# A first attention whose keys are projected for two heads at once, and whose probabilities are transposed by VectorE and DMA instead of TensorE

## The chip, the cores and the metric

The kernel runs on one core of one Trainium2 chip. The metric is the device time of one execution in microseconds, the median over repeated runs. A core has TensorE (PE; its weight loads are shown as PEld), VectorE (DVE), ScalarE (ACT), GpSimd (POOL) and SyncE (SP), which here only issues transfers. Each engine works through its own instructions in order and waits at semaphores for the others.

## The reference

Four layers, each an attention and a feed-forward network, with a layer norm behind each. Only the first attention matters here: 1024 rows of 256, 16 query heads and 4 key and value heads of 128, a window of 64 keys, and a difference of two softmaxes, one over each half of the head's 128 dimensions.

```python
q = q * cos + _rotate_half(q) * sin
k = k * cos + _rotate_half(k) * sin
...
q1, q2 = (q[..., :sub], q[..., sub:])
k1, k2 = (k[..., :sub], k[..., sub:])
attn1 = jnp.einsum('bhqd,bhkd->bhqk', q1, k1) * scale
attn2 = jnp.einsum('bhqd,bhkd->bhqk', q2, k2) * scale
...
a1 = jax.nn.softmax(attn1.astype(jnp.float32), axis=-1).astype(x.dtype)
a2 = jax.nn.softmax(attn2.astype(jnp.float32), axis=-1).astype(x.dtype)
diff = jax.nn.relu(a1 - lam.reshape(1, H, 1, 1) * a2)
diff = diff / (diff.sum(axis=-1, keepdims=True) + 1e-06)
out = jnp.einsum('bhqk,bhkd->bhqd', diff, v)
out = out.transpose(0, 2, 1, 3).reshape(B, S, H * hd)
return out @ Wo
```

## The kernel before

Eight stages run one after the other; `attn0` is the first. It works in 32 units: for each key head g (0 to 3) the eight row tiles t of 128 rows. A unit takes the four query heads of g for 128 rows, in two blocks b of 64 rows, each against a window of 128 keys, and in two pairs r of heads. Queries and keys lie transposed, with 64 of the head's dimensions on partitions 0 to 63 and again 64 on partitions 64 to 127: the two heads of a pair take one half of the partitions each. So both halves need the same key rows, and before the change the weight Wk is laid out with each 64 columns twice, so that the projection itself fills both halves.

The loop in `attn0` (from L621) makes iteration i out of parts of several units. It writes the order for PE, ACT, DVE and POOL by hand (`in_order`); SP's queue is ordered by the scheduler. In iteration i stand, in this order:
- the PE transposes of unit i - 3 into a PSUM bank (L729) and ACT's copy to `pt` (L731)
- `attn0_probs`, second part, for unit i - 1: three small DVE operations (L700 to L702), four differences (L708) with ACT's relu behind each (L712)
- one piece of work ahead (`operands`, `rotated`): a projection on PE (L154) and its product with the cosine and sine table on DVE (L570 for Q, L572 for K). After two such pieces POOL subtracts and adds (L577, L578). A run of four units holds six pieces, for the next run's K and two pairs of Q: one per iteration and a second one in odd iterations
- for g = 0, V's tile t (`make_values`), and its copies shifted by 64 rows, two transfers on SP
- the values of unit i - 3 (L735) and ACT's copy of them to `ot` (L741)
- the scores of unit i: mask matmuls (L666) and sixteen products of 64 partitions (L676) into a `wide` PSUM tile, DVE's maximum over it (L684), eight exponentials on ACT (L692)
- the second piece ahead, in odd iterations
- `attn0_probs`, third part, for unit i - 1: two small DVE operations (L716, L718) and POOL's product with the reciprocal sums (L720)
- Wo for unit i - 3 (L747) and the sum into x on DVE (L235)

The second attention (`attn1`) already transposes its probabilities in squares of 32 on DVE (`turn_probs`, L276) and moves them to their partitions with transfers on SP (L284). After the units, the layer norm runs in two halves, its output goes to DRAM (`moe_rows`), and the weights of the first experts are loaded (`gu`, `wd`).

Of the kernel before, what the change touches and what calls it, by code (L numbers as in the profile page):

```python
# [28 lines left out]
ALU = mybir.AluOpType  # L29
AX = mybir.AxisListType  # L30

P = 128
T = 1024
NT = T // P
D = 256
NC = D // P
HALF = 512
PAD = 64
# [474 lines left out]
def attn0(k, a):  # L513

    nc = k.nc
    window_masks(k)
    table = k.tile("rope", [P, 2, T])
    wk, wq, wo = [None] * 2, [None] * 4, [None] * 4

    def load_keys(i):
        wk[i] = k.weights(
            [P, NC, 512],  # L530
            a["L0_attn_Wk"][:, i * 512 : (i + 1) * 512].rearrange("(c p) f -> p c f", p=P),
        )

    def load(g):
        cols = slice(g * 512, (g + 1) * 512)
        wq[g] = k.weights(
            [P, NC, 512], a["L0_attn_Wq"][:, cols].rearrange("(c p) f -> p c f", p=P)
        )
        wo[g] = k.weights(
            [P, 4, D], a["L0_attn_Wo"][cols, :].rearrange("(h p) m -> p h m", p=P)  # L540
        )

    load_keys(0)
    for i, n in enumerate(("rope_cos", "rope_sin")):
        nc.sync.dma_start(out=table[:, i, :], in_=a[n])
    load(0)
    wv = k.weights([P, NC, 512], a["L0_attn_Wv"].rearrange("(c p) f -> p c f", p=P))

    lam = k.tile("rope", [P, 4, 2], tag="lam", bufs=1)
    for pair in range(2):  # L550
        nc.sync.dma_start(
            out=lam[pair * 64 : pair * 64 + 64],
            in_=a["L0_attn_lam"].rearrange("(g p r) -> g p r", g=4, p=2)[:, pair, :]
            .unsqueeze(0).to_broadcast([64, 4, 2]),
        )
    nc.vector.tensor_scalar(lam, lam, -1.0, None, ALU.mult)
    load_keys(1)
    load(1)

    def rotated(weight, half, first, second, scale):  # L560

        parts = []
        for i in range(2):
            ps = k.bank()
            k.project(ps, lambda c: weight(i, c), half * HALF, HALF)
            t = k.tile("t", [P, 2, HALF])
            twice = ps.unsqueeze(1).to_broadcast([P, 2, HALF])
            by = table[:, :, half * HALF : (half + 1) * HALF]
            if scale == 1.0:
                nc.vector.tensor_tensor(t, twice, by, ALU.mult)  # L570
            else:
                nc.vector.scalar_tensor_tensor(t, twice, scale, by, ALU.mult, ALU.mult)  # L572
            parts.append(t.rearrange("p i (b n) -> p i b n", n=64))
            if i == 0:
                yield
        x, y = parts
        nc.gpsimd.tensor_tensor(first, x[:, 0], y[:, 1], ALU.subtract)  # L577
        nc.gpsimd.tensor_tensor(second, y[:, 0], x[:, 1], ALU.add)  # L578
        yield

    keys, queries = {}, {}

    def operands(g, half):

        if half == 0:
            keys[g] = [k.tile("k", [P, PAD + T]) for _ in range(2)]
            for kt in keys[g]:
                nc.gpsimd.memset(kt[:, :PAD], 0.0)
        cols = slice(PAD + half * HALF, PAD + (half + 1) * HALF)
        yield from rotated(  # L590
            lambda i, c: wk[g // 2][:, c, (g % 2 * 2 + i) * P : (g % 2 * 2 + i + 1) * P],
            half, *(kt[:, cols].rearrange("p (b n) -> p b n", n=64) for kt in keys[g]), 0.125,
        )

        queries[g, half] = [k.tile("q", [P, 8, 2, 64]) for _ in range(2)]
        for pair in range(2):
            yield from rotated(
                lambda i, c: wq[g][:, c, (2 * pair + i) * P : (2 * pair + i + 1) * P],
                half, *(q[:, :, pair, :] for q in queries[g, half]), 1.0,
            )  # L600

    odd, even = [], []

    def make_values(t):
        vt = k.tile("v", [P, 512])
        ps = k.bank()
        k.project_rows(ps, lambda c: wv[:, c, :], t * P)
        nc.scalar.copy(vt, ps)  # L610
        odd.append(vt)
        vt = k.tile("v", [P, 512])
        if t == 0:
            nc.gpsimd.memset(vt[:64], 0.0)
        else:
            nc.sync.dma_start(out=vt[:64], in_=odd[t - 1][64:])
        nc.sync.dma_start(out=vt[64:], in_=odd[t][:64])
        even.append(vt)

    runs = [(g, half) for g in range(4) for half in range(2)]  # L620
    with k.in_order():  # L621
        for _ in operands(*runs[0]):
            pass
        units = [(g, t) for g in range(4) for t in range(NT)]
        ahead, made = iter(()), {}
        for i in range(len(units) + 3):
            ending = iter(())
            if i >= 3:
                g, t = units[i - 3]
                ending = attn0_values(k, t, g, made.pop(i - 3), (even, odd), wo[g])  # L630
            next(ending, None)
            if i - 1 in made:
                next(made[i - 1])
            if i < len(units):
                g, t = units[i]
                if t % 4 == 0:
                    for _ in ahead:
                        pass
                    at = i // 4 + 1
                    ahead = operands(*runs[at]) if at < len(runs) else iter(())  # L640
                    if t == 0 and 0 < g < 3:
                        load(g + 1)
                next(ahead, None)
                if g == 0:
                    make_values(t)
            next(ending, None)
            if i < len(units):
                made[i] = attn0_probs(k, t, g, queries[g, t // 4], keys[g], lam)
                next(made[i])
                if i % 2:  # L650
                    next(ahead, None)
            if i - 1 in made:
                made[i - 1] = next(made[i - 1])
            for _ in ending:
                pass
# [65 lines left out]
    yield four  # L721


def attn0_values(k, t, g, four, values, wo):

    nc = k.nc
    ps = k.bank()
    for i in range(4):
        nc.tensor.transpose(ps[:, i * P : (i + 1) * P], four[:, i, :], k.ident)  # L729
    pt = k.tile("pt", [P, 2, 2, P])  # L730
    nc.scalar.copy(pt.rearrange("p r b n -> p (r b n)"), ps)  # L731
    yield
    out = k.bank()
    for b in range(2):
        nc.tensor.matmul(  # L735
            out[:, b * 256 : (b + 1) * 256].rearrange("p (r n) -> p r n", r=2),
            lhsT=values[b][t][:, g * P : (g + 1) * P], rhs=pt[:, :, b, :],
            start=True, stop=True,
        )
    oT = k.tile("ot", [P, 4, 2, 64])  # L740
    nc.scalar.copy(  # L741
        oT.rearrange("p h b n -> p b h n"), out.rearrange("p (b h n) -> p b h n", b=2, n=64)
    )
    yield
    y = k.bank()[:, :D]
    for i in range(4):
        nc.tensor.matmul(  # L747
            y, lhsT=oT[:, i % 2 * 2 + i // 2].rearrange("p b n -> p (b n)"), rhs=wo[:, i, :],
            start=i == 0, stop=i == 3,
        )  # L750
    k.add_rows(t, y)
# [1344 lines left out]
def ffn3(k, a):  # L2096
# [46 lines left out]


STAGES = (attn0, ffn0, attn1, ffn1, attn2, ffn2, attn3, ffn3)
SCOPES = {
    attn0: dict(wide=2, mask=1, rope=1, k=4, v=16, q=4, t=4, e=3, diff=4, pt=3, ot=3),
    ffn0: dict(wide=0, gu=1, wd=1, route=8, rows=6, xT=3, s=3, h=3, hT=3, y=4, prep=1),
    attn1: dict(q=2, k=5, v=12, pt=2, p4=2, turned=2, ot=7, bv=1, prep=1),
    ffn1: dict(p4=4, t2=15, parts=2),  # L2150
# [39 lines left out]
def laid_out(inputs):  # L2190

    a = {n: np.asarray(v) for n, v in inputs.items()}
    a["L0_attn_x"] = a["L0_attn_x"].reshape(T, D)
    a["rope_cos"], a["rope_sin"] = rope_tables()


    wq = a["L0_attn_Wq"].reshape(D, 8, 2, 2, 64)
    a["L0_attn_Wq"] = wq.transpose(0, 1, 3, 2, 4).reshape(D, 2048)
    wk = a["L0_attn_Wk"].reshape(D, 4, 2, 1, 64)
    a["L0_attn_Wk"] = np.broadcast_to(wk, (D, 4, 2, 2, 64)).reshape(D, 1024)  # L2200
    for n in ("bq", "bk", "bv"):
        a[f"L1_attn_{n}"] = a[f"L1_attn_{n}"].reshape(16, P).T
    for n in ("w_gate_up", "w_proj"):
# [44 lines left out]
```

## Time and profile before

| | |
|---|---|
| median of three runs | 2282.05 us (2280.4 to 2284.7) |
| the profiled execution | 2276.97 us |
| its span | 2275.3 us |
| mean granted TensorE clock | 0.965 |
| PE busy | 2065.0 us, 91% of the span |
| DVE busy | 1325.2 us, 58% |
| ACT busy | 856.9 us, 38% |
| POOL busy | 528.2 us, 23% |
| first maximum of the first attention (L684) starts | 28.42 us |
| last one starts | 272.32 us |
| last sum into x (L235) starts | 294.04 us |

The times in the table by engine are sums of busy time over the whole span, over stages with different limits. A row of a group gives the line, the engine, the operation, the tile written and the tile read, the shapes, the count, then busy us and mean ns of one, then the idle time of the engine before them and who ended it. The chain of waits follows the work that ended last back from the end: each row is a start, a length and what was running.

### The profile page before, as it was taken

What the parts mean: (1) busy time and instruction counts of PE and PEld (TensorE: products, weight loads), DVE (VectorE), ACT (ScalarE), POOL (GpSimd) and SP (SyncE); (2) the same over time, 40 slices, a digit from 0 to 9 for tenths busy, and PEclk for the clock granted to TensorE, in tenths of its full rate; (3) what the DMA queues carried; (4) which work ended last, traced back from release to release, by engine and by line L of the source; (5) the groups of instructions that cost most, each with busy time, mean ns of one, the idle gap of its engine ahead of it and who ended that gap; (6) DMA issues with size and microseconds to landing.
All of it is one profiled execution on the core that took longest, in us unless ns stands there. A gap on an engine that the chain in (4) does not pass through costs nothing.

```text
span 2275.3 us, 25208 instructions
## 1 busy us (share of the span) xinstructions
PE 2065.0 (91%) x7955; PEld 1211.8 (53%) x7955; DVE 1325.2 (58%) x2687; ACT 856.9 (38%) x2230; POOL 528.2 (23%) x805
## 2 busy tenths in 40 slices
PE   8999769799999997988888999899998778999997
PEld 4666545466676665754434444466666444444443
DVE  5677646567776777456744444476767774222223
ACT  3666624443343433444452224544443321111111
POOL 4333221333333333402110001333333220000000
PEclk9999879899999999979999999999999989999999
DMA  4100054254545544105000010244445441111100
GB/s 160 36 10 29 29 169 121 65 136 110 139 112 151 151 111 117 38 28 177 2 2 10 28 29 1 48 90 111 96 103 112 104 95 39 37 40 44 30 2 19
DMA packets 200804, 166.74 MB, mean 73 GB/s; under 512 B 71680, under 2 KB 176192, under 8 KB 200672
## 3 DMA queue, kind: packets, MB, share of 16 engines
q1 hardware_dynamic: 191088, 140.07, 24.0%
q0 software_dynamic: 9584, 25.05, 3.7%
q8 instruction: 65, 1.06, 0.2%
q14 instruction: 67, 0.55, 0.1%
HBM read 68.72 MB, written 17.17 MB: 38 GB/s over the span
## 4 chain that ended last, share of the span: by engine, by line
PE 67%; DVE 15%; ACT 6%; DMA 4%; issue 4%; POOL 2%; SPq 1%; DVEq 0%; ACTq 0%; POOLq 0%
PE bank L154 23%; PE wide L307 8%; PE wide L332 8%; PE bank L298 7%; PE bank L161 4%; DVE turned L276 3%; ACT e L692 3%; PE bank L758 2%; DMA pt<-turned 2%; PE bank L1107 2%; PE bank L1544 1%; PE bank L938 1%; PE bank L1282 1%; DVE st L684 1%; PE bank L747 1%
## 5 line engine op out<-in xcount | busy, mean ns | idle before, releaser
L154 PE MATMUL bank<-xT,w 128*128 128x512 f32 (+2 forms) x1520 | 659.8, 567 | 4.1 <-DVE xT L180 2.6
L154 PEld LDWEIGHTS bank<-xT,w 128*128 128x128 f32 (+1 forms) x1520 | 287.9, 194 | 272.6 <-issue 250.7
L276 DVE STREAM_TRANSPOSE turned<-p 128x128 f32<-128x128 f32 (+7 forms) x256 | 312.8, 1222 | 122.1 <-DMA pt<-turned 87.0
L307 PE MATMUL wide<-k,q 128*128 128x512 f32 (+3 forms) x768 | 294.1, 493 | 29.6 <-ACT p L253 28.7
L261 POOL TENSOR_SCALAR p<-p,st 128x128 f32<-128x128 f32 (+7 forms) x256 | 190.4, 744 | 503.0 <-DVE st L260 502.5
L298 PE MATMUL bank<-pt,v 128*128 128x256 f32 x1216 | 282.0, 375 | 7.5 <-DMA pt<-turned 5.0
L298 PEld LDWEIGHTS bank<-pt,v 128*128 128x128 f32 x1216 | 231.5, 194 | 61.9 <-issue 20.0
L307 PEld LDWEIGHTS wide<-k,q 128*128 128x128 f32 x768 | 141.2, 191 | 152.2 <-issue 93.6
L248 DVE TENSOR_REDUCE st<-wide 128x1 f32<-128x128 f32 (+7 forms) x256 | 194.1, 758 | 8.8
L253 ACT ACTIVATE p<-wide,st,factor 128x128 f32<-128x128 f32 (+7 forms) x128 | 106.4, 831 | 235.0 <-POOL st L250 223.7
L2138 DVE TENSOR_TENSOR t<-t,bank 128x512 f32<-128x512 f32 (+1 forms) x66 | 45.4, 688 | 251.6 <-PE bank L154 251.0
L332 PE MATMUL wide<-t,w 128*128 128x512 f32 (+1 forms) x392 | 187.3, 600 | 4.5 <-DVE t L2139 2.8
L253 ACT ACTIVATE p<-wide,st 128x128 f32<-128x128 f32 (+7 forms) x128 | 94.9, 741 | 249.5 <-DVE st L248 229.4
L2137 ACT ACTIVATE t<-bank 128x512 f32<-128x512 f32 (+1 forms) x66 | 39.4, 597 | 306.2 <-PE bank L154 306.2
L161 PE MATMUL bank<-w,xT 128*128 128x512 f32 (+3 forms) x320 | 124.6, 525 | 2.9 <-DVE xT L180 2.9
L243 DVE TENSOR_TENSOR wide<-wide,causal 128x128 f32<-128x128 f32 x256 | 74.2, 290 | 89.7 <-PE wide L307 88.5
L332 PEld LDWEIGHTS wide<-t,w 128*128 128x128 f32 (+1 forms) x392 | 68.2, 189 | 108.6 <-issue 48.1
L692 ACT ACTIVATE e<-wide,st 128x128 f32<-128x128 f32 x256 | 90.1, 377 | 50.9 <-DVE st L684 34.4
L1569 ACT ACTIVATE pt<-wide 128x1024 f32<-128x1024 f32 (+3 forms) x96 | 75.7, 811 | 72.2 <-PE wide L1563 69.9
L161 PEld LDWEIGHTS bank<-w,xT 128*128 128x128 f32 x320 | 59.2, 208 | 48.5 <-issue 42.7
L2131 POOL COPY t<-select 99x128 bf16<-99x128 bf16 (+1 forms) x33 | 9.4, 292 | 319.8 <-PE bank L988 319.8
L235 DVE TENSOR_TENSOR x<-bank,x 128x256 f32<-128x256 f32 x120 | 48.1, 412 | 50.6 <-PE bank L747 21.1
(310 smaller groups left out, 2864.0 us busy)
## 6 DMA issues: line engine op xcount, KB each, us to landing
pt<-turned SPq DMA_DIRECT2D x96, 128.0 KB, 2.8
pt<-turned SPq DMA_DIRECT2D x96, 96.0 KB, 2.4
pt<-turned SPq DMA_DIRECT2D x32, 256.0 KB, 4.9
w<-in_L_ffn_gate_up_dram SPq DMA_DIRECT2D x16, 512.0 KB, 3.7
pt<-turned SPq DMA_DIRECT2D x64, 112.0 KB, 2.5
pt<-turned SPq DMA_DIRECT2D x32, 224.0 KB, 4.4
w<-in_L_attn_Wq_dram SPq DMA_DIRECT2D x12, 512.0 KB, 4.3
w<-in_L_attn_Wo_dram SPq DMA_DIRECT2D x12, 512.0 KB, 3.8
```

The costliest lines, as they stand in the source:

```text
L154: self.nc.tensor.matmul(out, lhsT=weight(c), rhs=self.xcols(c, lo, n), start=c == 0, stop=c == NC - 1)
L161: self.nc.tensor.matmul(out, lhsT=self.xcols(c, lo, n), rhs=weight(c), start=c == 0, stop=c == NC - 1)
L243: nc.vector.tensor_tensor(scores[:, n - P : n], scores[:, n - P : n], self.causal, ALU.add)
L248: nc.vector.tensor_reduce(top, scores[:, :n], axis=AX.X, op=ALU.max, negate=True)
L253: nc.scalar.activation(probs[:, :n], scores[:, :n], AF.Exp, bias=top, scale=1.0 if scale is None else scale, accum_out=total,)
L261: self.nc.gpsimd.tensor_scalar(probs[:, :n], probs[:, :n], total, 1.0, ALU.mult, ALU.mult)
L276: nc.vector.transpose(squares[:, slot if both else 0], probs[:, :n].rearrange("p (k i b) -> p b k i", b=4, i=32),)
L298: self.nc.tensor.matmul(out[:, first * P :].rearrange("p (s q) -> p s q", q=32), lhsT=value, rhs=pt[:, first * 4 :, b * 32 : b * 32 + 32], ...
L307: self.nc.tensor.matmul(s[:, lo : lo + m], lhsT=query, rhs=key(lo, m), start=True, stop=True)
L332: nc.tensor.matmul(acc[m][:, half * HALF : (half + 1) * HALF], lhsT=down[:, m * P : (m + 1) * P], rhs=h, start=i == 0, stop=i == count - 1,)
L692: nc.scalar.activation(e[:, r, f, b, :], sc[:, r, f, b, :], AF.Exp, bias=top[:, at : at + 1], accum_out=total[:, at : at + 1],)
L1569: nc.scalar.activation(two[:, :, lo:], sc[:, :, lo:], AF.Exp)
```

## The change

There are three parts.

K: Wk is laid out without the doubling, so one projection holds one half of the dimensions of two key heads, one on each half of the partitions. `rotated` is called for K only when g is even, and makes both heads' keys; POOL subtracts and adds for each head on its own 64 partitions (four operations in place of two). Four transfers on SP then copy each head's keys to the other 64 partitions. Wk is one load of 512 KB instead of two, and `k` has six buffers instead of four.

Probabilities: `attn0_turned` is new. It transposes a unit's probabilities in 32x32 squares on DVE, with the rows read at a stride, and four transfers of 64 KB on SP spread the result to `pt`. It is called in iteration i for unit i - 2, after the differences of unit i - 1. The PE transposes and ACT's copy are gone, and the matmul of the values reads `pt` in blocks of 32.

Order: since there is no copy ahead of the values any more, `attn0_values` starts directly with its matmuls, at the place where they stood.

```diff
-    load_keys(0)
+    wk = k.weights([P, NC, 512], a["L0_attn_Wk"].rearrange("(c p) f -> p c f", p=P))
...
-    load_keys(1)
     load(1)
...
         x, y = parts
-        nc.gpsimd.tensor_tensor(first, x[:, 0], y[:, 1], ALU.subtract)
-        nc.gpsimd.tensor_tensor(second, y[:, 0], x[:, 1], ALU.add)
+        for rows, out in first:
+            nc.gpsimd.tensor_tensor(out, x[rows, 0], y[rows, 1], ALU.subtract)
+        for rows, out in second:
+            nc.gpsimd.tensor_tensor(out, y[rows, 0], x[rows, 1], ALU.add)
         yield
...
+        heads = range(g, g + 2) if g % 2 == 0 else ()
         if half == 0:
-            keys[g] = [k.tile("k", [P, PAD + T]) for _ in range(2)]
-            for kt in keys[g]:
-                nc.gpsimd.memset(kt[:, :PAD], 0.0)
...
+        if heads:
+            cols = slice(PAD + half * HALF, PAD + (half + 1) * HALF)
+            own = [slice(j * 64, j * 64 + 64) for j in range(2)]
+            yield from rotated(
+                lambda i, c: wk[:, c, (g + i) * P : (g + i + 1) * P], half,
+                *(
+                    [
+                        (own[j], keys[g + j][f][own[j], cols].rearrange("p (b n) -> p b n", n=64))
+                        for j in range(2)
+                    ]
+                    for f in range(2)
+                ),
+                0.125,
+            )
+            for j in range(2):
+                for f in range(2):
+                    kt = keys[g + j][f]
+                    nc.sync.dma_start(out=kt[own[1 - j], cols], in_=kt[own[j], cols])
...
-            next(ending, None)
             if i - 1 in made:
                 next(made[i - 1])
+            if i - 2 in made:
+                made[i - 2] = attn0_turned(k, made[i - 2])
...
+def attn0_turned(k, four):
+    turned = k.tile("turned", [P, 4, P])
+    k.nc.vector.transpose(
+        turned.rearrange("p b (k q) -> p b k q", q=32),
+        four.rearrange("p k (i b) -> p b k i", b=4),
+    )
+    pt = k.tile("pt", [P, 4, 2, 2, 32])
+    for at in range(4):
+        k.nc.sync.dma_start(
+            out=pt[:, at].rearrange("p r b q -> p (r b q)"), in_=turned[at * 32 : at * 32 + 32]
+        )
+    return pt
...
-    ps = k.bank()
-    for i in range(4):
-        nc.tensor.transpose(ps[:, i * P : (i + 1) * P], four[:, i, :], k.ident)
-    pt = k.tile("pt", [P, 2, 2, P])
-    nc.scalar.copy(pt.rearrange("p r b n -> p (r b n)"), ps)
-    yield
...
-            out[:, b * 256 : (b + 1) * 256].rearrange("p (r n) -> p r n", r=2),
-            lhsT=values[b][t][:, g * P : (g + 1) * P], rhs=pt[:, :, b, :],
-            start=True, stop=True,
+            out[:, b * 256 : (b + 1) * 256].rearrange("p (r a q) -> p r a q", r=2, a=4),
+            lhsT=values[b][t][:, g * P : (g + 1) * P],
+            rhs=pt[:, :, :, b, :].rearrange("p a r q -> p r a q"), start=True, stop=True,
...
-    attn0: dict(wide=2, mask=1, rope=1, k=4, v=16, q=4, t=4, e=3, diff=4, pt=3, ot=3),
+    attn0: dict(wide=2, mask=1, rope=1, k=6, v=16, q=4, t=4, e=3, diff=4, turned=2, pt=3, ot=3),
...
-    a["L0_attn_Wk"] = np.broadcast_to(wk, (D, 4, 2, 2, 64)).reshape(D, 1024)
+    a["L0_attn_Wk"] = wk.transpose(0, 1, 3, 2, 4).reshape(D, 512)
```

More of the change, by code (lines that the diff above doesn't have):

```diff
@@ L525, in attn0 @@
     table = k.tile("rope", [P, 2, T])
[L526 to L532, printed above, removed]
+    wq, wo = [None] * 4, [None] * 4
     def load(g):
@@ L583, in operands @@
     def operands(g, half):
+        heads = range(g, g + 2) if g % 2 == 0 else ()
         if half == 0:
-            keys[g] = [k.tile("k", [P, PAD + T]) for _ in range(2)]
-            for kt in keys[g]:
-                nc.gpsimd.memset(kt[:, :PAD], 0.0)
[L589 to L593, printed above, removed]
+            for j in heads:
+                keys[j] = [k.tile("k", [P, PAD + T]) for _ in range(2)]
+                for kt in keys[j]:
+                    nc.gpsimd.memset(kt[:, :PAD], 0.0)
+        if heads:
[16 more added lines that the diff above has]
+                    nc.sync.dma_start(out=kt[own[1 - j], cols], in_=kt[own[j], cols])
         queries[g, half] = [k.tile("q", [P, 8, 2, 64]) for _ in range(2)]
@@ L598, in operands @@
                 lambda i, c: wq[g][:, c, (2 * pair + i) * P : (2 * pair + i + 1) * P],
-                half, *(q[:, :, pair, :] for q in queries[g, half]), 1.0,
+                half, *([(slice(0, P), q[:, :, pair, :])] for q in queries[g, half]), 1.0,
             )
@@ L721, in attn0_probs, with attn0_values @@
     yield four
-def attn0_values(k, t, g, four, values, wo):
-    nc = k.nc
-    ps = k.bank()
-    for i in range(4):
-        nc.tensor.transpose(ps[:, i * P : (i + 1) * P], four[:, i, :], k.ident)
-    pt = k.tile("pt", [P, 2, 2, P])
-    nc.scalar.copy(pt.rearrange("p r b n -> p (r b n)"), ps)
-    yield
+def attn0_turned(k, four):
[10 more added lines that the diff above has]
+    return pt
+def attn0_values(k, t, g, pt, values, wo):
+    nc = k.nc
     out = k.bank()
@@ L2198, in laid_out @@
     a["L0_attn_Wq"] = wq.transpose(0, 1, 3, 2, 4).reshape(D, 2048)
-    wk = a["L0_attn_Wk"].reshape(D, 4, 2, 1, 64)
-    a["L0_attn_Wk"] = np.broadcast_to(wk, (D, 4, 2, 2, 64)).reshape(D, 1024)
+    wk = a["L0_attn_Wk"].reshape(D, 2, 2, 2, 64)
+    a["L0_attn_Wk"] = wk.transpose(0, 1, 3, 2, 4).reshape(D, 512)
     for n in ("bq", "bk", "bv"):
```

## The prediction

> **What bounds the kernel now.** The change touches only the first attention stage, the first 296 us of the 2275 us span, so I read that stage alone. First its busy times in a table by stretch (the columns are length, then busy us and instruction count of PE, PEld, DVE, ACT and POOL, then the granted TensorE clock, the DMA share and GB/s):
>
> ```profile
> 130.00:165.00 35.00, 32.57 (x187) 21.50 (x186) 27.24 (x55) 23.02 (x119) 13.85 (x12) 1.00 0.00 1
> ```
>
> PE is busy for 93% of this stretch and DVE for 78%. That looks like a PE bound, but an average hides who ends the wait. So next I read the chain of waits of the stage in order of time (start, length, what). Three pieces show three kinds of interval between the exponentials of two units:
>
> ```profile
> 36.67 2.91 ACT e L692 x16
> 40.22 1.14 DVE diff L708 x4
> 41.36 1.13 DVE t L570
> 42.49 1.14 DVE st L684
> ...
> 147.93 2.91 ACT e L692 x16
> 151.08 1.26 DVE st L701
> 152.37 0.97 DVE st L702
> 153.63 0.87 DVE diff L708 x3
> 154.50 1.14 DVE t L572
> 155.64 1.13 DVE st L684
> ...
> 156.86 1.23 ACT e L692 x7
> 158.16 1.61 ACT e L692 x9
> 160.29 1.13 PE bank L735 x4
> 161.75 0.89 PE wide L676 x16
> ```
>
> The first piece is a ring of DVE and ACT: exponentials, 0.64 of small DVE work, difference (1.14), rotation (1.13), maximum (1.17 to the next exponential). It closes in 36.67 to 43.66, that is 6.99 us. The second piece is the same ring, 8.93 us long, because two tiny operations (L701, L702), 0.16 each elsewhere, took 1.26 and 0.97 while POOL was at its rotations and its product. The third goes through PE: exponentials, the copy of the transposed probabilities behind them on ACT, values (L735), scores (L676), maximum: 156.86 to 164.01, 7.15 us. A fourth kind, PE's own queue, takes 7.87. The starts of the 32 maxima (L684) run from 28.42 to 272.32, 243.9 us, and repeat every four units as 8.94, 7.14, 7.87, 7.14 = 31.1. So DVE with ACT and PE are nearly equal rings, and work on DVE is not free.
>
> Third, the groups by line and shape for the prices, and the page's DMA issues for the new transfers:
>
> ```profile
> L570 DVE TENSOR_TENSOR t<-bank,rope 128x1024 f32<-128x1024 f32 x32 | 38.8, 1221 | 9.5 <-PE bank L154 9.5
> L729 PE MATMUL bank<-ident,diff 128*128 128x128 f32 x128 | 20.2, 282 | 0.0
> L731 ACT COPY pt<-bank 128x512 f32<-128x512 f32 x32 | 19.5, 608 | 7.3 <-PE bank L729 7.3
> L276 DVE STREAM_TRANSPOSE turned<-p 128x512 f32<-128x512 f32 x32 | 35.5, 1110 | 13.4 <-DMA pt<-turned 8.5 <-POOL p L261 4.8
> ...
> pt<-turned SPq DMA_DIRECT2D x96, 96.0 KB, 2.4
> ```
>
> L276 is the second attention's transposition by squares, with the same shape and pattern that the change brings to the first: 1.11 us on DVE.
>
> **Removed.** Per unit, the four PE transposes (0.60 together) and ACT's copy (0.61). Of sixteen K projections eight go: 8 x 1.72 = 13.8 us of PE and 8 x 1.22 = 9.8 us of DVE. With the transposes PE loses 20.2 + 13.8 = 34 us. ACT's copy was a link of the 7.15 ring, so that ring disappears.
>
> **Added on DVE.** 32 transpositions. In the order of the changed program each stands after the differences of the unit before and ahead of the rotation and the maximum of the next. That is inside the 6.99 ring. Price 1.11 plus two semaphore waits of 0.05 (seen before L276) = 1.2. The bounds are 0, if PE makes DVE wait there anyway, and 1.2; I take 1.2, since PE is what gets lighter. Behind the transposition wait the rotation, the maximum, ACT's exponentials and PE's later scores. An interval with a rotation becomes 6.99 + 1.2 = 8.2; one without, 8.2 - 1.14 = 7.06.
>
> **Moved on POOL.** K's rotation becomes four operations on 64 partitions in place of two on 128. POOL casts of 64x128 and 128x128 take 0.29 alike, so I price each at the 1.27 of a full one (lower bound half). Total work stays (16 x 1.27), but one block of 5.1 us stands where 2.5 stood. It starts as the rotation ends, 1.1 before the exponentials, and at 40.6 in the clock of the first piece it would still run when L701 wants to start at 39.8, and the product L720 queues behind it. So L701 waits 0.7 and L702 0.9: 1.6 per K block. The Q block at the end of such a run costs the 1.9 seen in the second piece. Without a K block the run has four rotations instead of six, and its last Q block ends before L701: no delay.
>
> **Added on SP.** 128 transfers pt<-turned and 16 copies of K halves; one 512 KB weight load goes. In the second attention SP's issue rows for pt<-turned have a median of 0.60, and the transfer lands 2.4 after the issue begins: 3 x 0.6 + 2.4 and two hand-overs of 0.1, 4.4 after the transposition. Counted back from the next maximum through scores, mask and values (2.25), the values are needed 7.1 after it where the intervals have rotations, and 4.8 after it where they have none. So the latency is covered, by 2.7 and by 0.4 us. The queue behind SP (V's halves, attention weights) stands in an order where each waits for work no later than the transposition that follows it, so I price that at nothing; a 512 KB load ahead of a set could cost 1.7 us, inside the 2.7. K's copies land some 3 us after POOL's block and are used two units later; at the start they fall in the wait for lam (landing at 20.13), so the head stays.
>
> **The sum over the intervals.** By the four units that share a run of rotations, new against old, in us:
> Units 1 to 3: 7.0 + 9.8 + 8.2 = 25.0 against 21.1. Units 4 to 7: 10.1 + 8.2 + 8.2 + 7.06 = 33.6 against 34.9. Units 8 to 11: 31.7 against 31.1. Units 12 to 15: 4 x 8.2 + 1.6 = 34.4 against 31.1. Units 16 to 19: 32.8 + 1.9 + 1.6 = 36.3 against 31.1. Units 20 to 23: 33.6 against 31.4. Units 24 to 27: 31.7 against 30.8. Units 28 to 31, no rotations: 4 x 7.06 = 28.2 against 32.4.
> Together 254.4 against 243.9: +10.5.
>
> **PE's clock.** The last run was dear before for another reason:
>
> ```profile
> 247.00:249.00 2.00, 0.10 (x3) 0.09 (x1) 2.00 (x6) 1.75 (x9) 0.00 (x0) 1.00 0.72 234
> 251.00:253.00 2.00, 1.33 (x6) 0.73 (x4) 1.28 (x6) 1.52 (x7) 0.00 (x0) 0.50 0.00 0
> ```
>
> PE stood for 1.9 us, then ran at clock 0.50, and one interval took 9.59. The excess of the last run over 4 x 7.15 was 3.8. PE will stand still longer there (4.3 of 7.06 busy), so I add 3.8 again; bounds 0 and four times 2.4. The Trainium skill (TensorE: Matmul & The Clock Gate, Part 1: The HAM clock gate) puts the fall of the clock at one idle window of about 3.4 us; here it fell after a gap of 1.9, with shorter ones before. By that rule the gaps I expect (up to 2.4 us) would not throttle at all and the sum would be 3.8 lower.
>
> **Tail.** From the last exponential (273.64) to the last sum into x (294.04) it took 20.4. New, from that exponential: Wo of unit 29 to 8.4, its sum 9.0, the last transposition 10.2, landing 14.5, values, copy and Wo 4.3: 18.9; by way of unit 30, held by 768 KB of expert weights, 19.7. So -1, between -2.5 and +2.
>
> 10.5 + 3.8 - 1 = +13.3. The profiled execution took 2276.97 (span 2275.3 and 1.7 around it), 5 below the median of the runs, 2282.05. On it the sum gives 2290; on the median, **2295 us**.
>
> **Rivals.** (1) Faster: PE is the bound, and DVE waits for scores in any case, so the transposition fits in that wait. For it speak the 93% and the intervals of 7.87 and 9.59; against it, PE's work per unit falls to 6 to 7 us. Without 30 x 1.2 on the ring the sum is 13.3 - 36 + 1.5 (PE then bounds units 4 to 7) = -21: 2261. It decides once the transposition's share on the ring is under 0.76 us a unit (1.2 - 13.3 / 30). (2) Slower still: PE, with more gaps, loses its clock also in the four intervals without a rotation and twice more: 6 x 2.4 = 14 on top, 2309. For it: the clock at 0.50 after 1.9 us; against: 1.00 held from 130 to 245. (3) The transfers are late: at 4.9 us to landing, the page's row for 256 KB, the last run alone gets 4 x 1.2 more, 2300; with SP stalls in ten units 3 us each, 2325. (4) A wash: 64-partition operations on POOL take half and the clock holds: 13.3 - 4.8 - 3.8 = +5, 2287, with a shorter tail 2285.
>
> **The numbers.** This kernel can be told from no change at about 0.2%, 4.6 us. Forecast 0.60 (its own range 2288 to 2302: the clock's 0 to 3.8 and 5 more, the tail's bounds), rival 1 0.09, rival 2 0.12, rival 3 0.07, rival 4 0.12. Faster 0.10 (rival 1 and a little), same 0.13 (rival 4 and the low end of the forecast), slower 0.77. The range 2279 to 2308 leaves out rival 1, the worst of 2 and 3.
>
> **What would show it.** Right: the maxima's starts 8.2 apart with a rotation and 7.1 without, the transposition in the chain between difference and rotation, PE's busy time in the stage down by 34 us with no gain, L701 stretched after K blocks. Wrong: intervals near 7 with DVE idle ahead of the maximum until PE (rival 1); clock rows under 0.9 between 130 and 245 (rival 2); PE's values idle until pt<-turned (rival 3). A head longer by several us, or stages after 300 us that moved, would upset the sum too.

## The result, and the profile after

The changed kernel takes 2282.53 us, the median of 20 runs; the kernel before, beside it, takes 2280.4 us, also of 20. The ratio is 1.0006, 95% interval 0.9997 to 1.0015: no difference that can be told. The forecast was 2295 and slower. The medians differ by 2.1 us, the ratio makes it +1.4. The time lies inside the range given, but a slower kernel was forecast and none can be told; the chance given for that was 0.13.

The profiled execution of the changed kernel took 2287.66 us (span 2285.9). First the table of the same stretch as before (length, then busy us and count of PE, PEld, DVE, ACT, POOL, then PE's clock, DMA share, GB/s):

```profile
130.00:165.00 35.00, 29.33 (x136) 19.40 (x138) 27.66 (x56) 18.87 (x103) 14.12 (x12) 0.90 0.20 47
```

PE's busy share fell from 93% to 84%, and the granted clock, a mean over the stretch, from 1.00 to 0.90. DVE hardly moved (78% to 79%). Now the chain of waits of the stage (start, length, what):

```profile
125.70 2.91 ACT e L703 x16
...
130.38 1.05 DVE turned L740
131.43 1.11 DVE t L565
132.54 1.14 DVE st L695
...
133.76 2.91 ACT e L703 x16
...
136.91 1.00 DVE st L712
...
138.30 0.78 issue
...
143.27 2.91 ACT e L703 x16
```

The transposition (L740) stands in the chain between the differences and the rotation, as forecast. The ring from 125.70 to 133.76 is 8.06 long. It was 6.99, and the transposition with its hand-over is 1.05 of it. The next interval, behind a K block, is 9.51 long: L712 takes 1.00 where the interval before had 0.17, and the chain then shows 0.78 ahead of the last three differences, where it has 0.10 one interval earlier ("issue" is time in which the engine waits for nothing that the profile shows).

The 32 maxima now start from 27.95 to 277.28: 249.33 us against 243.9, +5.4. Summed over the runs of four units, in the order of the prediction: 24.74, 32.35, 31.23, 33.73, 34.77, 32.82, 31.01, 28.67. The tail from the last exponential to the last sum into x is 19.2 against 20.4, so that sum starts at 297.73 against 294.04, +3.7. The prices, from the groups by line and shape and the page's DMA issues:

```profile
L740 DVE STREAM_TRANSPOSE turned<-diff 128x512 f32<-128x512 f32 x32 | 35.1, 1098 | 0.0
L571 POOL TENSOR_TENSOR q<-t,t 128x512 f32<-128x512 f32 x16 | 20.3, 1269 | 70.1 <-DVE t L563 49.0 <-DVE st L727 21.2
L571 POOL TENSOR_TENSOR k<-t,t 64x512 f32<-64x512 f32 x8 | 10.1, 1263 | 25.7 <-DVE t L565 25.4
...
pt<-turned SPq DMA_DIRECT2D x224, 64.0 KB, 2.1
```

One loss in this execution was not seen again. Behind the feed-forward network the chain shows a wait that no other profile of this study has at that place:

```profile
424.82 5.62 another core or an unknown queue
```

The span of this profile is 10.6 us longer than that of the kernel before; the stage of the change makes 3.7 of it and this wait 5.6. A second profile of the same kernel, told below, is without the wait and took 2272.39 us. What it was stays open.

### The profile page after: what moved, and what is told of

It is laid out like the page before. It is cut to its first block, busy times and chain, and to the rows that moved or that the text cites. A ratio compares the mean times of both kernels' runs of the same rounds, so it can differ in the third digit from the quotient of the medians.

```text
span 2285.9 us, 25073 instructions
## 1 busy us (share of the span) xinstructions
PE 2050.6 (90%) x7795; PEld 1198.8 (52%) x7795; DVE 1339.4 (59%) x2711; ACT 840.3 (37%) x2198; POOL 529.6 (23%) x805
## 4 chain that ended last, share of the span: by engine, by line
PE 62%; DVE 19%; ACT 6%; DMA 4%; issue 4%; POOL 3%; SPq 2%; another core or an unknown queue 0%; DVEq 0%; ACTq 0%; POOLq 0%
PE bank L154 21%; PE wide L332 7%; PE wide L307 7%; PE bank L298 7%; DVE turned L276 4%; ACT e L703 3%; PE bank L161 3%; DMA pt<-turned 3%; PE bank L780 2%; PE bank L1566 2%; SPq L284 1%; DVE st L695 1%; DVE turned L740 1%; DVE diff L719 1%; PE bank L1129 1%
## 5 line engine op out<-in xcount | busy, mean ns | idle before, releaser
L154 PE MATMUL bank<-xT,w 128*128 128x512 f32 (+1 forms) x1488 | 647.6, 569 | 6.9 <-DVE xT L180 5.0
L154 PEld LDWEIGHTS bank<-xT,w 128*128 128x128 f32 x1488 | 287.3, 197 | 273.0 <-issue 247.9
L769 PE MATMUL bank<-w,ot 128*128 128x256 f32 x256 | 72.8, 434 | 26.7 <-ACT ot L763 26.6
```

Of the source, the lines that this page charges most:

```text
L154: self.nc.tensor.matmul(out, lhsT=weight(c), rhs=self.xcols(c, lo, n), start=c == 0, stop=c == NC - 1)
```

## The experiments

Theory: the change pays for the transposition in the ring of DVE and ACT, 1.05 us in every unit, and for a longer POOL block behind K; what it earns from PE is no more than that, for PE's rings of 7.14 and 7.87 stood only 0.15 and 0.88 above the ring of 6.99. Rivals: PE or its clock sets the pace (then DVE work is cheap); the landing of the transposed probabilities sets it (then their later use helps); the two halves of the change each do nothing. The kernel before was run again beside each of the three groups of experiments: 2275.32, 2274.46 and 2275.05 us. One per mille is 2.3 us, and a difference in us below is worked out from the ratio, not from two medians.

**The K part alone.** Unit i - 3 keeps its PE transposes and ACT's copy (`attn0_values` is that of the kernel before).

```diff
+            next(ending, None)
             if i - 1 in made:
                 next(made[i - 1])
-            if i - 2 in made:
-                made[i - 2] = attn0_turned(k, made[i - 2])
...
```

> Only the change of K: one projection for two heads, four POOL operations on 64 partitions, copies by SP; the PE transposes and ACT's copy stay as before. Theory A (both halves of the change move the time and cancel): the runs of four units with four rotations instead of six lose their PE-bound interval (7.87) and their POOL delay (1.8), about 2.5 us in each of four such runs; the three K blocks of four POOL operations delay L701 and L702 by 1.5 us each. Together some 6 us faster than before, about 2276 where before is 2282. Theory B (neither half matters, the stage is bound elsewhere): within 2 us of before. Theory C (K's copies by SP are late): PE waits for k ahead of scores, slower.

Measured: 2272.42 us, ratio 0.9986 (0.9971 to 1.0), that is -3.2 us. The maxima span 241.44 against 243.9. Half of what was expected: the 7.87 intervals did not vanish, one is left in most runs of four, and two of 8.76 came in. By the time alone this gain cannot be told from none.

**The transposition alone,** with the old K (`attn0_turned` and `attn0_values` are those of the changed kernel).

```diff
-            next(ending, None)
             if i - 1 in made:
                 next(made[i - 1])
+            if i - 2 in made:
+                made[i - 2] = attn0_turned(k, made[i - 2])
...
```

> Only the transposition by VectorE and SP; K projected for each head as before. Theory A: every interval with a rotation is 8.04 (6.99 + 1.05), all runs have six rotations and one POOL delay of 1.3 to 1.9: 33.5 per four units against 31.1, so 10 us over the stage, 1 us given back in the tail: 9 us slower than before, about 2291 where before is 2282. Theory B (the transposition is hidden): within 2 us of before or faster. Theory C (the transfers bound the stage): more than 20 us slower, with PE's values waiting for pt<-turned in most units.

Measured: 2283.18 us, ratio 1.0037 (1.0023 to 1.0051), +8.4 us. Nearly every run of four is 9.1, 8.05, 8.0, 8.05, and the maxima span 251.73, +7.8. So the halves are opposed, and the cost of this one is clear of the noise: +7.8 and -2.5 on the span of the maxima make +5.3, and the whole change shows +5.4 (+4.4 in its second profile). In the whole time they make +5.2 against +1.4, which their 95% intervals do not tell apart. The third rival is out.

**The transposition done twice.** In `attn0_turned`:

```diff
     k.nc.vector.transpose(turned..., four...)
+    k.nc.vector.transpose(turned..., four...)
```

> The changed kernel, with every transposition on VectorE done twice into the same tile (the second is superfluous). Theory A (the transposition lies whole in the ring of DVE and ACT): 30 intervals longer by 1.03 to 1.07 each, 31 us slower than the changed kernel, about 2313. Theory B (it is hidden behind PE): under 10 us slower.

Measured: 2311.47 us, ratio 1.0162 (1.0134 to 1.019). Against the changed kernel's 1.0006 that is 1.56%, 35 us; the span of the maxima grows by 281.57 - 249.33 = 32.2, or 1.07 for each of 30 units. Its chain of waits:

```profile
133.46 1.06 DVE turned L740
...
134.54 1.10 DVE turned L744
135.65 1.11 DVE t L565
```

The second one stands in the chain at its full length, as the first does. Nothing else was late enough to hide it, so PE does not set the pace of these intervals.

**K's rotation staged.** Two POOL operations on all 128 partitions write a tile `both`, and eight transfers on SP spread it to the keys.

```diff
+            both = [k.tile("both", [P, HALF]) for _ in range(2)]
...
-                *(
-                    [
-                        (own[j], keys[g + j][f][own[j], cols].rearrange("p (b n) -> p b n", n=64))
-                        for j in range(2)
-                    ]
-                    for f in range(2)
-                ),
-                0.125,
+                *([(slice(0, P), s.rearrange("p (b n) -> p b n", n=64))] for s in both), 0.125,
...
-                    kt = keys[g + j][f]
-                    nc.sync.dma_start(out=kt[own[1 - j], cols], in_=kt[own[j], cols])
+                    for rows in own:
+                        nc.sync.dma_start(out=keys[g + j][f][rows, cols], in_=both[f][own[j]])
```

> The changed kernel, but POOL makes the rotated keys of two heads with two operations on 128 partitions into a tile of their own, and eight copies by SP instead of four bring them to their places. Theory A (the long POOL block delays L712 and L713): the three intervals of 9.5 become 8.04, 4.5 us faster than the changed kernel, about 2278 where that is 2282.5; POOL busy 10 us less. Theory B (the 9.5 has another cause, such as K's projection): the intervals stay at 9.5.

Measured: 2271.24 us, ratio 0.9984 (0.997 to 0.9999). Against the changed kernel -0.22%, 5 us. The three intervals behind K blocks fall from 9.53 to 8.0, and POOL's busy time falls by 11.6 us. In the groups the small operation is the changed kernel's L712 (first row) and this kernel's L706 (second):

```profile
L712 DVE TENSOR_TENSOR st<-st 128x4 f32<-128x4 f32 x32 | 9.5, 296 | 1.1
```

```profile
L706 DVE TENSOR_TENSOR st<-st 128x4 f32<-128x4 f32 x32 | 6.5, 202 | 1.1
```

3.0 of the 5 us is this one operation, no longer stretched; most of the rest is the wait of the differences behind it. So the price of the K block lies in POOL's four operations, at full price each.

**The same on the kernel with the K part alone.**

> Before with only K changed and K staged in that way; PE transposes and ACT's copy stay. Theory A: the three intervals of 8.5 of the kernel with K alone become 7.1, 4 us less than that one, so 7 us faster than before. Theory B (the copies of K cost as much as they save): the same as before.

Measured: 2271.32 us, ratio 0.9982 (0.9964 to 1.0): -4.1 against before, 1 better than the K part alone where 4 were expected, and the 95% intervals do not tell the two apart. The delays behind K blocks are gone, but the intervals are 7.15 to 7.87 all the same, with a few of 8.7. Its chain of waits at one of those:

```profile
111.60 0.48 ACT pt L735
...
112.13 2.08 PE bank L739 x4
```

ACT's copy and PE end the wait here, with PE slowed (the same values took 1.13 at 97.11). With the PE transposes left in place, this ring takes over what the others give up.

**The transposition moved, values at i - 3.** The call goes behind the maximum of unit i and the third part of unit i - 1, so that it no longer stands ahead of the next exponentials.

```diff
-            if i - 2 in made:
-                made[i - 2] = attn0_turned(k, made[i - 2])
...
             if i - 1 in made:
                 made[i - 1] = next(made[i - 1])
+            if i - 2 in made:
+                made[i - 2] = attn0_turned(k, made[i - 2])
```

> The changed kernel with the transposition of unit i - 2 moved behind the maximum of unit i on VectorE, under its exponentials, and the values still at i - 3. Theory A (the transposition is in the ring, the transfers are hidden by the 7 us between it and the values): the ring is shorter by 1.05, but the values now need the transfer at once, and it lands 4.1 after the transposition; intervals become 9 to 10 through transfer, values, scores, maximum, 30 to 50 us slower than the changed kernel. Theory B (transfers never matter): 30 us faster than the changed kernel.

Measured, in a single execution: 2379.48 us, some 105 above the kernel before. The direction was expected, the size is twice to three times as large. The chain of waits:

```profile
145.75 1.10 DVE turned L740
...
148.76 2.10 DMA pt<-turned
...
151.00 2.04 PE bank L757 x4
...
154.95 1.23 DVE st L695
```

A new ring: transposition, SP's issues, landing, values, scores, maximum, 10.7 us long from one transposition to the next (156.48); over the stage the maxima stand 11.1 apart in the mean. PE idles in it, its clock over 130 to 165 is 0.75, and the values take 2.04 where the last unit of the changed kernel shows 1.11. That PE slows down in a ring that idles it is a part of the size that was missed: values, mask and scores take some 1.6 more per interval than at full clock.

**The values at i - 4, the transposition where the change put it.**

```diff
-        for i in range(len(units) + 3):
+        for i in range(len(units) + 4):
...
-            if i >= 3:
-                g, t = units[i - 3]
-                ending = attn0_values(k, t, g, made.pop(i - 3), (even, odd), wo[g])
+            if i >= 4:
+                g, t = units[i - 4]
+                ending = attn0_values(k, t, g, made.pop(i - 4), (even, odd), wo[g])
```

> The changed kernel with the values taken from unit i-4 instead of i-3, the transposition left where it was, ahead of the rotation and the maximum. It tells apart what the gain of late_lag4 came from: the place of the transposition or the later use of its result. If the transposition in the ring is the price (my theory), the intervals stay at 8.05 with a rotation and 6.9 without, only the 7.93 of unit 28 may fall to 6.9, the tail grows by one iteration (2 to 4 us), and the time is that of the changed kernel, 2280 to 2286 (ratio to the kernel before 0.999 to 1.003). If the landing of the transposed probabilities is what the changed kernel pays for (rival), the intervals fall towards 7.05 and the time towards 2262 (ratio 0.993).

Measured: 2277.39 us, ratio 1.001 (0.9999 to 1.0021). The intervals stay at 8.04 and 6.9, the span of the maxima at 249.18, and the tail grows from 20.5 to 22.9, counted from the last maximum. Using the result later earns nothing by itself: the second rival is out, the landing was covered in nearly every interval.

**Both: moved, and the values at i - 4.** The edits of the last two together.

> As the kernel before it, but the values, Wo and the sum of a unit one iteration later (i - 4). Theory A: the ring is 7.0 with a rotation and 5.9 without, PE then bounds some intervals at 7 to 7.9, POOL's delays stay; 25 us off the intervals, 2 to 4 given back by a longer tail: 2258 where the changed kernel is 2282. Theory B (the transposition is not in the ring, the loss comes with the transfers or the K copies): within 5 us of the changed kernel.

Measured: 2261.58 us, ratio 0.9928 (0.9902 to 0.9955), -16 us. Against the changed kernel that is -18, where 24 were expected. The intervals fall to 7.05 and 5.91; behind the K blocks they are 8.6, and at the start of most runs of four 8.2 to 10.0. Two of these are PE's: the chain of 9.20 (unit 8) and of 10.04 (unit 24) runs through Wo and a projection on PE, at a granted clock of 0.60 over 204 to 208 and 0.69 over 208 to 214 in the second case (Wo took 3.78 there, 1.73 at full clock in the kernel before). With the transposition out of the ring, PE's slow clock does cost time. The move needs the extra unit of slack, and the slack alone is worth nothing.

**Both, with K staged.**

> The same with the rotated keys of two heads made by two POOL operations on 128 partitions into a tile of their own and copied by SP. Theory A: the three K blocks delay nothing any more, 4.5 us less than the kernel above, about 2254 where before is 2280. Theory B: no gain over before.

Measured: 2251.63 us, ratio 0.9888 (0.9862 to 0.9913), -25 us; it beats both kernels. The maxima span 219.44, 12 less than without the staging where 4.5 were expected; only part of it lies behind K blocks, for unit 24 alone takes 7.05 instead of 10.04, at clock 1.00. That PE kept its clock there is not shown to come from the staging. Its table by stretch and its chain of waits:

```profile
130.00:165.00 35.00, 31.42 (x168) 20.58 (x164) 30.50 (x63) 22.71 (x123) 15.08 (x13) 1.00 0.39 96
```

```profile
132.49 2.91 ACT e L697 x16
...
136.03 1.14 DVE diff L713 x4
137.17 1.13 DVE t L563
138.30 1.14 DVE st L689
...
139.53 2.91 ACT e L697 x16
```

This is the old ring of 6.99 again, 7.04 long. The transposition runs on DVE while ACT takes its exponentials, out of the chain. DVE does one transposition more per interval than in the kernel before and is busy for 87%.

**The changed kernel once more,** for a second profile.

> The changed kernel unaltered, a second profiled execution. By the theory the intervals of the first attention repeat within 0.1 (9.5 to 9.8 behind a K block, 9.1 to 9.3 behind a Q block, 8.05 with a rotation, 6.9 without), the stage's maxima span 249 to 250 us, and the 5.6 us in which the chain waited at 424.8 for something outside the core are not there again. If that wait belongs to the change, it is there again within 2 us of the same place, after the sum into x. Ratio to the kernel before 0.999 to 1.002.

Measured: 2275.32 us, ratio 1.0005 (0.9993 to 1.0018). The maxima span 248.29; most intervals repeat within 0.1 or 0.2, but unit 4 took 10.27 (9.25 in the first profile), unit 20 9.15 (9.85) and unit 28 6.94 (7.93). In unit 4 of this profile PE had first waited for the landing of a transposition (to 48.24), ran at half pace (scores 1.71), and DVE's rotation then waited 1.28 for PE: one place where the transfers and the clock did cost about 1 us. The wait at 424.8 is not there. The last sum into x starts at 297.64 (297.73 in the first profile), but the first gather of the feed-forward network at 317.74, where it was 319.86 and, before, 316.09: PE's clock held longer in the routing between them (0.83 over 301 to 305, against 0.56). So how far the +3.7 reaches varies by 2 us from one execution to the next.

## Why the prediction was wrong, by its steps

The forecast sum was +13.3; the measured place to hold it against is the last sum into x, +3.7 and +3.6 in the two profiles, and of the whole +1.4 (-0.7 to +3.4). The mechanism held at each place. What failed is the size of three terms, all taken too dear.

- **The step "1.11 plus two semaphore waits ... = 1.2"** failed. The transposition adds 1.05 (1.00 in many units). Its semaphore wait appears in the chain beside the first difference, and the four differences with it still take 1.14 (129.24 to 130.38). Units with a rotation stand at 8.05, those without at 6.92, against 8.2 and 7.06: some 4.4 us over 30 units. The forecast had put the bounds at 0 and 1.2 and taken the upper one; the lower neighbour in the trace, the 1.11 of the instruction itself, was nearer.
- **The step "so I add 3.8 again" for PE's clock** failed. The last run took 28.67 and 27.68, not 28.2 + 3.8. The clock did fall: in the first profile PE waited for the landing behind the transposition of 247.68, and ran the mask in 0.54 and the scores in 1.74, at half pace (0.32 and 0.89 in the kernel before at full clock):

```profile
247.68 1.01 DVE turned L740
...
250.58 2.10 DMA pt<-turned
...
254.24 0.54 PE wide L677
254.78 1.74 PE wide L687 x16
```

  That cost 1.0 in one interval, and nothing in the second profile, where the clock was 0.50 over 247 to 249:

```profile
247.00:249.00 2.00, 2.00 (x18) 1.81 (x16) 2.00 (x5) 1.60 (x9) 0.00 (x0) 0.50 0.00 0
```

  PE has 3.9 us of work per interval there at full clock (7.85 busy in the 13.8 us from 262.4 to 276.2). The clock record shows 0.5 for 3.4 us in each of the two profiles, which adds 1.7 at most, so a slow PE fits into 6.9. The forecast carried over the price of a slow PE from a kernel in which PE was the late one; before, the chain of that run goes through PE at half pace:

```profile
248.91 2.56 PE bank L747 x8
...
253.06 2.07 PE bank L735 x4
```

- **The Q block behind a K block, 1.9,** measured 1.2, 1.1 and 1.8 in the first profile, 1.6 us less over three, and 1.1 twice in the second; its third, 2.2, holds the wait for PE told above.
- Together 4.4 + 2.8 + 1.6 make 8.8 of the 9.6 us between +13.3 and +3.7 in the first profile; an earlier first maximum (27.95 against 28.42) gives 0.5.
- **The balance of the stage,** estimated from the intervals: the transposition put 30 x 1.05 = 31.5 us on the ring, and four intervals lost their rotation, 4 x 1.14 = 4.6. The bare ring of before, 27 x 6.99 and 4 x 5.85 (6.99 less a rotation), 212.1 in all, left 31.8 of the 243.9 to waits for PE, its clock, ACT's copy and POOL; that of the changed kernel, 6.99 + 22 x 8.04 + 8 x 6.90 = 239.1 (1.05 more in 30 of them), leaves 10.2 of 249.33, of which the K blocks make 4.5. 31.5 - 4.6 - 21.6 = +5.3. So what the change takes off the other rings did earn about two thirds of what the transposition costs.
- **Right:** the place of the transposition; that PE's lighter load brings no gain on balance (its busy time over the first 300 us fell from 261.0 to 239.8 and 237.9, not by 34; the mean clock over 28 to 270 fell from 0.98 to 0.93 and 0.94, which stretches some 230 us of work by about 10); the full price of 64-partition operations on POOL (1263 ns against 1269), though one of the two casts it was read from took another type, and like casts of 128x128 took 344 and 370 ns; 1.5 behind a K block against 1.6; 0.15 or less in the runs without one; the landing 4.0 after the transposition against 4.4, hidden but for about 1 us in one interval of each profile; the tail, -1.2 and -0.9 against -1.
- **Rival 1** (PE bounds, 2261) is excluded by the doubled transposition. That the kernel with the transposition out of the ring took 2261.58 is a coincidence of numbers: against the kernel before beside it that is -16, for another reason. **Rival 2** was half right: the clock fell, to a mean of 0.90 in both profiles over 130 to 200 where it had been 1.00, but the intervals there, 8.05 and 6.92, show no time lost by it; the chains show a loss of about 1 in the last run of the first profile and in unit 4 of the second. **Rival 4** (2287, from a clock that costs nothing and POOL at half price) came near the number; its first half held, its second did not, so that nearness is partly luck.

The Trainium skill (TensorE: Matmul & The Clock Gate, Part 1: The HAM clock gate) was weighed with its single idle window of about 3.4 us. The sum by it, with no loss of clock, was the nearer one. But its reason did not hold here: between 130 and 200 the longest gap in PE's records was 3.1 us and the mean clock was 0.90, because the clock stood at 0.50 in three stretches (from 141.05 and 158.12 for 3.4 us, from 175.18 for 6.8 us).

What stays open: why the whole shows +1.4 where the stage shows +3.7. The interval reaches to +3.4, and the clock in the routing gives back 2 us in one profile of two; no run isolates it.

## What to carry to other kernels

Before counting what an edit removes from the busiest engine, find which ring ends each interval: here PE, 93% busy in the stretch shown, lost over 20 us of busy time and the stage did not get shorter, because 1.05 us a unit came into the ring of two other engines. Work that nobody awaits soon belongs behind the instruction that releases the next engine, and it needs enough units between it and its use to cover its transfers; either half of that alone lost time or earned none, both together gained 0.7%. When a term comes from a neighbouring row, take the instruction's own duration, and ask whether the wait or the slow clock that cost something there is still late here.

## What the runs showed that was not expected

- A POOL operation on 64 partitions took as long as one on 128 (1263 and 1269 ns); a split by partitions doubled the block. The forecast had priced it so, on thin evidence.
- PE's mean clock over 130 to 165 went to 0.90 with PE busy 84% and gaps of up to 3.1 us, to 0.75 at 67% busy in the 10.7 us ring, and was 1.00 again in the fastest version (90% busy). The clock record of these profiles holds 1.0 and 0.5 alone, so the means are shares of time at half pace. Neither the busy share nor the longest gap decides by itself: over 165 to 200 the fastest version had PE busy 84% too, and a gap of 3.0 us, at clock 1.00. The ring of 10.7 us that idles PE also slows the part of it that PE does.
